# A two-layer decoder on one core: when expert lists are fetched, how constants are summed, and the order at the end of a feed-forward

## The chip, the cores and the metric

The kernel runs on one core of one Trainium2 chip. A core has TensorE (PE in the profile, with its weight loads as PEld), VectorE (DVE), ScalarE (ACT), GpSimd (POOL) and SyncE (SP), which here only issues transfers. The metric is the device time of one execution in microseconds. Before the change three runs gave a median of 3037.61 us (3037.56 to 3045.76).

## What is computed

A decoder of two layers works on x of shape (4, 512, 512): 4 batches, 512 tokens, 512 features. Each layer has self-attention, cross-attention and a feed-forward, and each of the six is added to x and normalised. The change lies in layer 0's feed-forward, a mixture of eight experts of which each token uses two:

```
h = x @ down_w + down_b
probs = softmax(x @ router_w + router_b - COST_LAMBDA * cost)
topv, topi = top_k(probs, 2);  gate = softmax(topv)
out = zeros
for k in range(2):
    mask = one_hot(topi[..., k], 8)
    acc = zeros
    for e, (w1, b1, w2, b2) in enumerate(experts):       # hidden sizes 256 512 768 1024, twice
        hm = h * mask[..., e:e + 1]
        acc = acc + (gelu(gelu(hm) @ w1 + b1) @ w2 + b2)
    out = out + acc * gate[..., k:k + 1]
out = out + 0.1 * (gelu(gelu(h) @ shared_w1 + shared_b1) @ shared_w2 + shared_b2)
out = out @ up_w + up_b
out = out + (gelu(x) @ core_w + core_b)
x = layernorm(x + out)
```

A token that an expert doesn't get still receives that expert's constant, `gelu(b1) @ w2 + b2`, as its masked input is zero. So the sum over all experts is one constant row, plus, for the two chosen experts, the difference between the true product and that constant.

## The kernel before, in words

All arithmetic around the change is in 32-bit floats; the trace shows each product of such operands as two matmul records ("passes"). The residual x stays in 16 tiles of 128 tokens by 512. PSUM tiles of one bank come from three rings that matter here: three `ps_s`, two `ps_t` (for transposes and small products), three `ps_m`.

The program is written in a tile language. A scheduler in it decides at compile time, from its own model, in which order each engine's queue holds its instructions: roughly source order, but an instruction that its model holds back is passed by later ones. Each engine then works through its own queue. The body of a runtime branch (`tc.If`) is scheduled as a block of its own. `mm` (L156, its matmuls are recorded at L160) and `add_projection` (L287, its adds at L292) are helpers used everywhere.

The feed-forward `l0_ffn` (L502) goes as follows.

- `hidden(b)` (L532) transposes a batch of x, makes `gelu(h)` for its 512 tokens and `gelu(x)`. `logits(b)` (L547) computes the router and a long chain of small VectorE operations: softmax, ranks, counts, gates. `send(b)` (L596) turns ranks into places and scatters each token's `gelu(h)` row to the lists of its two experts in HBM (`hidden_of`), by eight indirect transfers from GpSimd. `core(b)` (L627) adds `gelu(x) @ core_w` to the residual: 32 matmul passes of 512 columns, whose results VectorE adds to x (L292), four PSUM tiles a batch. `shared_expert(b)` (L681) is the expert that every token uses. The calls are written out from L742 on in the order hidden(0), logits(0), core(0), hidden(1), send(0), logits(1), shared_expert(0), hidden(2), send(1), logits(2), core(1), shared_expert(1), hidden(3), send(2), logits(3), shared_expert(2), send(3), the rotary angles, loads of experts 1 to 3, shared_expert(3).
- `add_bias` (L772) adds the output biases to x on GpSimd.
- The lists, from L776: expert e takes the first 512 rows of its list as one block. `fetch` (L697) loads them from HBM into the single buffer `ctx`, issued by SP and waiting for the scatters. `turn` (L707) transposes them (matmuls at L712, copies at L714 and L716). `block` (L733) runs the expert's hidden chunks of 128: `first(j)` (L636) multiplies by w1, ScalarE takes the gelu, VectorE subtracts gelu(b1); `second(j)` (L648, matmuls at L656) multiplies by w2 and accumulates. `run_pieces` (L671) puts each chunk's `second` behind the next chunk's `first`, so that TensorE has work while the gelu runs. Behind the second `first` of a block it calls `turn` for the next list. Results go back to HBM by SP (`store`, L719). The fetch of list e+1 is written ahead of block e.
- Behind every second expert there is a runtime branch (L793) for the rows past 512 of the two lists. It was entered for experts 6 and 7 only (the trace has their 384-row blocks between 918 and 963 us). Behind it stand the loads of the experts two pairs on (L804): after expert 1 those of 4 and 5, after expert 3 those of 6 and 7.
- `add_every(e)` (L736) adds expert e's constant to the row `every`: for each chunk of 128 hidden units one product of a single column of gelu(b1) with a 128x256 chunk of w2. In total 40 chunks.
- The end, from L806: `every` is turned into a column, GpSimd gathers each token's two result rows (32 indirect transfers, L817, eight a batch), `core(2)` and `core(3)` follow.
- `finish(b)` (L823) scales the first row by its gate on ScalarE (L827), adds the second on VectorE (L828), transposes, adds the constant and the shared expert (L833), projects by `up_w` onto x (16 passes) and normalises. `finish(0)` is called before layer 1's attention; that attention calls `finish(1)`, `finish(2)` and `finish(3)` after its heads 0, 1 and 2 (`at_start`).

Layer 1's attention, `l1_attn` (L843), runs 64 heads. While head n is finished, head n+1 is scored (`scores`, L893: product, causal mask, maximum, exponential) and the queries of head n+2 are projected and rotated (`queries`, `rope`; the last step of the rotation is on GpSimd, L860). `turn` (L913) transposes probabilities, `values` (L925) multiplies them by v and ends in a copy on ScalarE. A quarter of the time the keys of the next group are projected (`keys`, L875). `layernorm` (L215) takes bn_stats and bn_aggr of four tiles on VectorE, a root on ScalarE, a reciprocal and four scalings on VectorE.

Of the kernel before, what the change touches and what calls it, by code (L numbers as in the profile page):

```python
# [86 lines left out]
def decoder_kernel(ctx: ExitStack, tc: tile.TileContext, a: dict, out: bass.AP):  # L87
# [206 lines left out]
    def chunks(w):  # L294
        return [w[:, k, :] for k in range(w.shape[1])]
# [203 lines left out]

    def l0_ffn():  # L502
        slots = [cp.tile([P, T // P], I32, tag=f"slot{k}", name="slot") for k in range(2)]
        share = [cp.tile([P, T // P], F32, tag=f"share{k}", name="share") for k in range(2)]
# [8 lines left out]
        V.tensor_copy(b_down, ps[:, :L])  # L513
        G.tensor_tensor(cub, cub, ub, ALU.add)
        G.memset(run, 0.0)
        b1g = cp.tile([P, N_HCH], F32, tag="b1g", name="b1g")
        A.activation(b1g, bc[:, B_E1:B_E1 + N_HCH], AF.Gelu)
        gh, shared = [weight(), weight()], [weight(), weight()]
        base = {e: B_E1 + sum(HID[:e]) // P for e in range(N_EXP + 1)}
        st, rt, scatters, now = {}, {}, [], {}  # L520
# [213 lines left out]
            run_pieces(products(e, n, [y[:, :n] for y in x], store(e, start, n)), between)  # L734

        def add_every(e):  # L736
            w2 = experts[e][1]
            ps, at = pst(), base[e] - B_E1
            mm(ps[:1, :L], [b1g[:, at + i:at + i + 1] for i in range(w2.shape[1])], chunks(w2))
            V.tensor_tensor(every, every, ps[:1, :L], ALU.add)  # L740

        hidden(0)  # L742
        logits(0)
# [1 line left out]
        hidden(1)  # L745
        send(0)
        logits(1)
        shared_expert(0)
        hidden(2)
        send(1)  # L750
        logits(2)
        core(1)
        shared_expert(1)
        hidden(3)
        send(2)
        logits(3)
        b2 = ap.tile([N_EXP + 1, L], F32, tag="bias", name="b2", bufs=2)
        nc.sync.dma_start(b2, a["b2_rows"])

        every = prob("cos", [S], 1)[:1, :L]  # L760
        ps = pst()
        PE.matmul(ps[:1, :L], lhsT=kc[:N_EXP + 1, C_B2W:C_B2W + 1], rhs=b2, start=True, stop=True)
        V.tensor_copy(every, ps[:1, :L])
        shared_expert(2)
        send(3)
        all_angles()
# [6 lines left out]
            for x in X:  # L773
                G.tensor_tensor(x, x, cub, ALU.add)

        turned = {0: turn(fetch(0, 0, BLOCK), BLOCK)}  # L776
        add_bias()
        for e in range(N_EXP):
            ahead = {}
            if e + 1 < N_EXP:  # L780
                got = fetch(e + 1, 0, BLOCK)
                ahead[1] = lambda: turned.update({e + 1: turn(got, BLOCK)})
            block(e, 0, BLOCK, turned.pop(e), ahead)
            if 0 < e < N_EXP - 1:
                add_every(e + 1)
            if e % 2 == 0:
                continue
            flush()

            got = act("xT", [2, MORE // P, L])  # L790
            more = [fetch(e - 1 + i, BLOCK, MORE, got[:, i]) for i in range(2)]
            most, *count = nc.values_load_multi_w_load_instructions(counts[0:1, 3 * (e // 2):3 * (e // 2) + 3])[1]
            with tc.If(most > BLOCK):  # L793
                for i in range(2):
                    with tc.If(count[i] > BLOCK):
                        x = turn(more[i], MORE)
                        block(e - 1 + i, BLOCK, MORE, x)
                        flush()
                        with tc.If(count[i] > BLOCK + MORE):
                            for start in range(BLOCK + MORE, ROOM, MORE):  # L800
                                n = min(MORE, ROOM - start)
                                block(e - 1 + i, start, n, turn(fetch(e - 1 + i, start, n), n, x))
                                flush()
            experts.update((i, load_expert(i)) for i in range(e + 3, min(e + 5, N_EXP)))  # L804

        everyT = cp.tile([P, 2], F32, tag="everyT", name="everyT")  # L806
        for m in range(2):
            ps = pst()
            PE.matmul(ps[:, :1], lhsT=every[:, tk(m)], rhs=ones[:1, :1], start=True, stop=True)
            V.tensor_copy(everyT[:, m:m + 1], ps[:, :1])  # L810

        results = {}
        for b in range(B):
            y = results[b] = weight((4, 2, L))
            for t in range(4):
                for k in range(2):
                    G.indirect_dma_start(out=y[:, t, k, :], out_offset=None, in_=result_of[:],  # L817
                                         in_offset=bass.IndirectOffsetOnAxis(
                                             ap=slots[k][:, 4 * b + t:4 * b + t + 1], axis=0))
        core(2)  # L820
        core(3)

        def finish(b):  # L823
            y, o = results.pop(b), prob("ctx", [2, S], 1)
            for t in range(4):
                g1, g2 = (x[:, 4 * b + t:4 * b + t + 1] for x in share)
                A.activation(y[:, t, 0, :], y[:, t, 0, :], AF.Copy, scale=g1)  # L827
                V.scalar_tensor_tensor(y[:, t, 0, :], y[:, t, 1, :], g2, y[:, t, 0, :], ALU.mult, ALU.add)  # L828
            for m in range(2):
                pt = pst()  # L830
                for t in range(4):
                    PE.transpose(pt[:, tk(t)], y[:, t, 0, tk(m)], ident)
                V.scalar_tensor_tensor(o[:, m, :], pt, everyT[:, m:m + 1], shared[m][:, cols(b)],  # L833
                                       ALU.add, ALU.add)
            add_projection(b, chunks(o), chunks(up_w))
            layernorm(b)

        return finish

# [575 lines left out]
```

## Time and profile before

| what | us |
|---|---|
| median of three runs | 3037.61 |
| the profiled execution, whole | 3051.64 |
| its span, first to last instruction | 3049.9 |
| TensorE busy in it | 2851.6 (93%) |
| VectorE busy | 1770.6 (58%) |
| ScalarE busy | 1061.9 (35%) |
| GpSimd busy | 342.5 (11%) |
| hidden, logits, send, shared expert, cores 0 and 1 | about 583 to 718 |
| first blocks of the eight lists | about 718 to 917 |
| rows past 512 of lists 6 and 7 | about 917 to 966 |
| cores 2 and 3, finish of batch 0, first transposes of layer 1 | about 966 to 1031 |
| first heads of layer 1, finish of batches 1 to 3 | about 1031 to 1127 |

The busy time of an engine is summed over the whole span and says little about a stage; the stages above have their own limits. A line of a timeline gives start, duration, engine, source line, operation, output and inputs, and how many instructions are merged in it; the bracket at its end gives the idle time of the engine before it and what released it. A queue line (SPq) is the issue of a transfer, not the transfer. A row of the table by stage has, for each engine, the busy time and in parentheses the number of instructions; behind the engines follow the granted clock of TensorE (1.00 is full), the busy share of the 16 DMA engines and GB/s.

### The profile page before, as it was taken

How to read it: one execution, taken by the hardware profiler on the slowest of the kernel's cores; microseconds unless marked ns; L12 is line 12 of the kernel's file. 1: busy time of each engine (PE TensorE's matmuls, PEld its weight loads, DVE VectorE, ACT ScalarE, POOL GpSimd, SP SyncE). 2: the span in 40 equal slices, each digit the busy share in tenths (PEclk: the TensorE clock that was granted, in tenths of full speed). 3: DMA queues.
4: the chain of work that ended last, by engine and by line, in shares of the span. 5: the costliest groups of instructions: out<-in, count | busy, mean ns of one | idle time of the engine just before them, and what ended most of it. 6: DMA issues, size and time to landing. Idle time of an engine off the chain costs nothing.

```text
span 3049.9 us, 30386 instructions
## 1 busy us (share of the span) xinstructions
PE 2851.6 (93%) x11514; PEld 1370.0 (45%) x11514; DVE 1770.6 (58%) x3585; ACT 1061.9 (35%) x1945; POOL 342.5 (11%) x294
## 2 busy tenths in 40 slices
PE   7999998998798899999999999999899998998988
PEld 3444444565455345545545555533233343332444
DVE  4565455443111477757766766755655655564898
ACT  2343243233112222323322232334545444444444
POOL 3000000042002201101100100111212012110000
PEclk9999998989999899999999999999899898999999
DMA  9600001013312120000000001200201100000000
GB/s 374 266 15 1 18 11 35 11 39 115 122 38 77 55 83 1 1 1 1 1 1 1 1 28 35 90 1 15 90 1 42 63 1 28 1 15 1 1 28 28
DMA packets 56454, 131.85 MB, mean 43 GB/s; under 512 B 4810, under 2 KB 24027, under 8 KB 50147
## 3 DMA queue, kind: packets, MB, share of 16 engines
q1 hardware_dynamic: 53218, 121.31, 10.9%
q0 software_dynamic: 3072, 8.39, 0.8%
q8 instruction: 99, 1.62, 0.2%
q14 instruction: 65, 0.52, 0.1%
HBM read 82.76 MB, written 46.92 MB: 43 GB/s over the span
## 4 chain that ended last, share of the span: by engine, by line
PE 52%; DVE 10%; POOL 2%; issue 2%; DMA 1%; ACT 1%; POOLq 0%; DVEq 0%; ACTq 0%; SPq 0%
PE ps_m L160 19%; PE ps_b L1116 7%; PE ps_m L887 6%; PE ps_s L900 5%; PE ps_m L1143 4%; PE ps_b L1132 2%; PE ps_t L917 2%; PE ps_m L932 2%; POOL q L860 1%; DVE maxes L1120 1%; DVE P L1335 1%; PE ps_m L1095 1%; DMA w<-in_L_ffn_downT 1%; PE ps_s L160 1%; DVE tmp L859 1%
## 5 line engine op out<-in xcount | busy, mean ns | idle before, releaser
L160 PE MATMUL ps_m<-w,attnT 128*128 128x512 f32 (+2 forms) x1216 | 446.0, 517 | 12.3 <-issue 8.0
L1120 DVE TENSOR_REDUCE maxes<-ps_b 128x2 f32<-128x1024 f32 x256 | 311.1, 1222 | 244.5 <-PE ps_b L1132 223.6
L1136 ACT ACTIVATE PT<-ps_b 128x1024 f32<-128x1024 f32 x256 | 261.5, 1024 | 313.5 <-PE ps_b L1132 312.9
L1132 PE MATMUL ps_b<-q,k 32*128 32x512 f32 x1024 | 306.4, 678 | 33.3 <-DVE maxes L1120 33.3
L1116 PE MATMUL ps_b<-k,q 32*128 32x512 f32 x1024 | 310.3, 665 | 0.9 <-DVE maxes L1120 0.5
L160 PEld LDWEIGHTS ps_m<-w,attnT 128*128 128x128 f32 x960 | 182.9, 193 | 193.0 <-issue 177.3
L887 PE MATMUL ps_m<-xT,w 128*128 128x512 f32 x512 | 260.3, 592 | 0.0
L292 DVE TENSOR_TENSOR x<-x,ps_m 128x512 f32<-128x512 f32 x128 | 88.0, 688 | 247.5 <-PE ps_m L160 244.6
L904 ACT ACTIVATE P<-ps_s,nmax 128x512 f32<-128x512 f32 (+3 forms) x256 | 135.2, 529 | 233.5 <-DVE nmax L902 232.4
L900 PE MATMUL ps_s<-k,q 128*128 128x512 f32 (+3 forms) x512 | 183.4, 441 | 18.4 <-POOL q L860 18.1
L1116 PEld LDWEIGHTS ps_b<-k,q 32*128 32x128 f32 x1024 | 87.1, 193 | 177.4 <-issue 141.0
L860 POOL TENSOR_TENSOR q<-tmp 128x512 f32<-128x512 f32 x64 | 81.3, 1270 | 750.8 <-DVE tmp L859 714.8
L932 PE MATMUL ps_m<-PT,v 128*128 128x512 f32 (+3 forms) x512 | 162.0, 439 | 2.4 <-DVE PT L920 2.3
L349 ACT ACTIVATE P<-ps_s,nmax 128x512 f32<-128x512 f32 x128 | 88.5, 693 | 204.1 <-DVE nmax L347 204.1
L1143 PE MATMUL ps_m<-PT,vv 128*32 128x512 f32 x1024 | 148.8, 655 | 5.8 <-ACT PT L1136 5.7
L160 PE MATMUL ps_m<-w,xT 128*128 128x512 f32 (+1 forms) x384 | 144.8, 533 | 8.1 <-DVE xT L235 4.2
L911 DVE TENSOR_SCALAR P<-P,sums 128x512 f32<-128x512 f32 (+3 forms) x256 | 145.5, 571 | 4.6
L932 PEld LDWEIGHTS ps_m<-PT,v 128*128 128x128 f32 x512 | 89.0, 190 | 103.5 <-issue 49.7
L917 PEld LDWEIGHTS ps_t<-kc,P 128*128 128x128 f32 x640 | 84.0, 141 | 114.3 <-issue 84.3
L327 PE MATMUL ps_m<-xT,w 128*128 128x512 f32 x256 | 122.2, 604 | 11.1 <-DMA w<-in_L_attn_Wq 11.1
L902 DVE TENSOR_REDUCE nmax<-ps_s 128x1 f32<-128x512 f32 (+3 forms) x256 | 125.2, 490 | 5.1
L160 PE MATMUL ps_m<-xT,w 128*128 128x256 f32 (+1 forms) x384 | 124.9, 463 | 0.8 <-DVE x L292 0.8
(266 smaller groups left out, 4290.9 us busy)
## 6 DMA issues: line engine op xcount, KB each, us to landing
hidden<-w SPq DMA_DIRECT2D x16, 1024.0 KB, 18.8
result<-w SPq DMA_DIRECT2D x16, 1024.0 KB, 19.0
w<-in_L_ffn_gateT SPq DMA_DIRECT2D x8, 1024.0 KB, 4.9
w<-in_L_ffn_upT SPq DMA_DIRECT2D x8, 1024.0 KB, 4.8
w<-in_L_ffn_downT SPq DMA_DIRECT2D x8, 1024.0 KB, 5.1
w<-in_L_attn_Wqkv SPq DMA_DIRECT2D x6, 1024.0 KB, 6.0
w<-in_L_attn_Wo SPq DMA_DIRECT2D x5, 1024.0 KB, 9.2
result<-P SPq DMA_DIRECT2D x18, 256.0 KB, 2.1
```

What stands on the lines that cost most here:

```text
L160: PE.matmul(ps, lhsT=x, rhs=y, start=(i == 0), stop=(i == n - 1))
L887: PE.matmul(ps_q[n], lhsT=wq[h // 4][:, i, tk(h % 4)], rhs=st["xt"][:, i, :], start=(i == 0), stop=(i == 3))
L900: PE.matmul(s[:, :w], lhsT=q[:, tk(qi)], rhs=k[:, :w], start=True, stop=True)
L904: A.activation(p[:, :w], s[:, :w], AF.Exp, bias=nmax[:, qi:qi + 1], accum_out=sums[:, qi:qi + 1])
L911: V.tensor_scalar(p[:, :w], p[:, :w], sums[:, qi:qi + 1], None, ALU.mult)
L917: PE.transpose(pt[:, tk(qi)], probs[qi][:, tk(c)], ident)
L932: PE.matmul(av[:, c * P:], lhsT=st["v"][:, c, tk(g)], rhs=pts[c][:, c * P:], start=(c == 0), stop=(c == 3))
L1116: PE.matmul(s[:, j, :], lhsT=q[strip(i), tk(qi)], rhs=k[strip(i), :], start=True, stop=True)
L1120: V.tensor_reduce(at[:, 2 * half:2 * half + 2, 16 * (1 - g % 2)], s, AX.X, ALU.max, negate=True)
L1132: PE.matmul(s[:, j, :], lhsT=k[strip(i), tk(c)], rhs=q[strip(i), :], start=True, stop=True)
L1136: A.activation(p, s, AF.Exp)
L1143: PE.matmul(avs[g][strip(i), :], lhsT=vv[c][:, 4 * m + i, 16 * par:16 * par + 32], rhs=pts[g, c, i // 2][:, i % 2, :], start=(c == 0), sto ...
```

## The change

Five edits in `l0_ffn`, one in how its end is scheduled.

1. `shared_expert(0)` is called behind `core(1)` instead of behind `logits(1)`, and `shared_expert(1)` behind `logits(3)` instead of behind `core(1)`.
2. `add_every` puts chunk i into the column strip i mod 4 of TensorE: 32 columns from column i of gelu(b1) on, so that row 32*(i mod 4) of the PSUM tile gets the chunk's product and the other 31 rows of the strip get products that nobody reads. The tile of gelu(b1) is 31 columns longer, cleared by GpSimd. `every` has 128 rows, cleared once by VectorE; up to four of them, a strip apart, hold partial sums.
3. The final transposition of `every` multiplies by a column that is 1 in the rows 0, 32, 64 and 96, which adds the partial sums.
4. A list is fetched right behind the `turn` of the preceding list, inside the preceding block, instead of ahead of the next block. In the branch for more than 896 rows, which was not entered, the rows go to another buffer than `ctx`.
5. `core(3)` is called inside `finish(0)`, behind its layernorm, instead of ahead of `finish(0)`.
6. From `core(2)` to the layernorm of batch 3 the queues of TensorE, VectorE and ScalarE are held in source order. The stretch contains `finish(0)`, `core(3)`, the start of layer 1's attention and its heads 0 to 2 with `finish(1)` to `finish(3)`. GpSimd and SP stay with the scheduler.

```
+    in_order = ExitStack()
...
-        b1g = cp.tile([P, N_HCH], F32, tag="b1g", name="b1g")
-        A.activation(b1g, bc[:, B_E1:B_E1 + N_HCH], AF.Gelu)
+        b1g = cp.tile([P, N_HCH + 31], F32, tag="b1g", name="b1g")
+        G.memset(b1g[:, N_HCH:], 0.0)
+        A.activation(b1g[:, :N_HCH], bc[:, B_E1:B_E1 + N_HCH], AF.Gelu)
...
         def add_every(e):
+
             w2 = experts[e][1]
-            ps, at = pst(), base[e] - B_E1
-            mm(ps[:1, :L], [b1g[:, at + i:at + i + 1] for i in range(w2.shape[1])], chunks(w2))
-            V.tensor_tensor(every, every, ps[:1, :L], ALU.add)
+            ps, at, nj = pst(), base[e] - B_E1, w2.shape[1]
+            for i in range(nj):
+                r = slice(32 * (i % 4), 32 * (i % 4) + 32)
+                PE.matmul(ps[r, :L], lhsT=b1g[:, at + i:at + i + 32], rhs=w2[:, i, :],
+                          start=(i < 4), stop=(i + 4 >= nj))
+            n = 32 * min(nj, 4)
+            V.tensor_tensor(every[:n], every[:n], ps[:n, :L], ALU.add)
...
         logits(1)
-        shared_expert(0)
         hidden(2)
         send(1)
         logits(2)
         core(1)
-        shared_expert(1)
+        shared_expert(0)
         hidden(3)
         send(2)
         logits(3)
+        shared_expert(1)
...
-        every = prob("cos", [S], 1)[:1, :L]
+        every = prob("cos", [S], 1)[:, :L]
+        V.memset(every, 0.0)
...
-        V.tensor_copy(every, ps[:1, :L])
+        V.tensor_copy(every[:1], ps[:1, :L])
...
-        turned = {0: turn(fetch(0, 0, BLOCK), BLOCK)}
+        turned, got = {}, {0: fetch(0, 0, BLOCK)}
+
+        def turn_next(e):
+            if e < N_EXP:
+                turned[e] = turn(got.pop(e), BLOCK)
+                if e + 1 < N_EXP:
+                    got[e + 1] = fetch(e + 1, 0, BLOCK)
+
+        turn_next(0)
         add_bias()
         for e in range(N_EXP):
-            ahead = {}
-            if e + 1 < N_EXP:
-                got = fetch(e + 1, 0, BLOCK)
-                ahead[1] = lambda: turned.update({e + 1: turn(got, BLOCK)})
-            block(e, 0, BLOCK, turned.pop(e), ahead)
+            block(e, 0, BLOCK, turned.pop(e), {1: lambda: turn_next(e + 1)})
...
-            got = act("xT", [2, MORE // P, L])
-            more = [fetch(e - 1 + i, BLOCK, MORE, got[:, i]) for i in range(2)]
+            rest = act("xT", [2, MORE // P, L])
+            more = [fetch(e - 1 + i, BLOCK, MORE, rest[:, i]) for i in range(2)]
...
-            PE.matmul(ps[:, :1], lhsT=every[:, tk(m)], rhs=ones[:1, :1], start=True, stop=True)
+            PE.matmul(ps[:, :1], lhsT=every[:, tk(m)], rhs=kc[:, C_ROW1:C_ROW1 + 1], start=True, stop=True)
...
+        in_order.enter_context(tc.manual_schedule(engines={nc.tensor.engine, nc.vector.engine, nc.scalar.engine}))
         core(2)
-        core(3)
...
             layernorm(b)
+            if b == 0:
+                core(3)
+            if b == B - 1:
+                in_order.close()
```

More of the change, by code (lines that the diff above doesn't have):

```diff
@@ L801, in l0_ffn @@
                                 n = min(MORE, ROOM - start)
-                                block(e - 1 + i, start, n, turn(fetch(e - 1 + i, start, n), n, x))
+                                block(e - 1 + i, start, n, turn(fetch(e - 1 + i, start, n, rest[:, i]), n, x))
                                 flush()
```

## The prediction, made before the changed kernel was built or run

> **What bounds the kernel now.** I read the page first, then the busy time by stage, then TensorE's timeline in the feed-forward, and for each gap there the queue it waited on. The page says TensorE carries the kernel: 93% busy. By stage, that breaks down once:
>
> ```profile
> 718.00:917.00 199.00, 170.50 (x606) 106.50 (x607) 32.50 (x62) 37.04 (x56) 0.00 (x0) 0.93 0.28 93
> 966.00:1031.00 65.00, 48.34 (x109) 21.51 (x110) 23.40 (x47) 11.04 (x21) 30.39 (x32) 0.86 0.41 136
> 1031.00:1127.00 96.00, 92.79 (x284) 46.76 (x284) 70.29 (x169) 28.79 (x65) 9.48 (x8) 0.99 0.19 66
> ```
>
> The columns are stretch, length, busy time of PE, PEld, DVE, ACT, POOL, then granted clock. TensorE is idle 28.5 of 199 us in the expert lists and 16.7 of 65 us at the feed-forward's end; then, in the first heads of layer 1, which finish batches 1 to 3, only 3.2 of 96. In the lists four gaps hold 26.3 us: before `turn` of lists 0 (6.15), 3 (5.28), 5 (10.43) and 7 (4.40). The queue of loads shows why for list 5:
>
> ```profile
> 820.93 3.62 PE L656 MATMUL ps_s<-w,k 128*128 128x256 f32 x16
> 834.98 1.94 PE L712 MATMUL ps_t<-kc,ctx 128*128 128x128 f32 x8 [10.43 <-DMA ctx<-hidden]
> 836.85 2.98 PE L160 MATMUL ps_t<-w,b1g 128*1 128x256 f32 x8
> ```
>
> ```profile
> 821.14 0.37 SPq L490 DMA_DIRECT2D w<-in_L_ffn_e_w  x1
> 821.62 0.41 SPq L491 DMA_DIRECT2D w<-in_L_ffn_e_w  x1
> 822.08 0.54 SPq L490 DMA_DIRECT2D w<-in_L_ffn_e_w  x1
> 822.66 0.66 SPq L491 DMA_DIRECT2D w<-in_L_ffn_e_w  x1
> 823.42 3.29 SPq L701 DMA_DIRECT2D ctx<-hidden  x1
> ```
>
> The list is fetched behind 3.5 MB of weights for experts 6 and 7. A gap costs more than itself: the eight passes at 834.98 take 1.94 us where eight elsewhere take 1.04. Stretches of 2 us show why, in the third column from the end: the granted clock falls to half about 4 us into the gap and stays there in the first work behind it.
>
> ```profile
> 825.00:827.00 2.00, 0.00 (x0) 0.00 (x0) 0.28 (x1) 0.00 (x0) 0.00 (x0) 1.00 1.06 373
> 829.00:831.00 2.00, 0.00 (x0) 0.00 (x0) 0.00 (x0) 0.00 (x0) 0.00 (x0) 0.50 1.04 363
> 835.00:837.00 2.00, 2.00 (x9) 1.60 (x10) 0.04 (x1) 0.59 (x1) 0.00 (x0) 0.50 1.09 384
> ```
>
> The end of the stage:
>
> ```profile
> 966.55 10.57 PE L160 MATMUL ps_m<-w,v 128*128 128x512 f32 x24
> 977.49 3.70 PE L160 MATMUL ps_m<-w,v 128*128 128x512 f32 x8 [0.37 <-issue]
> 984.56 5.40 PE L160 MATMUL ps_m<-w,attnT 128*128 128x512 f32 x8 [3.37 <-issue]
> 992.16 5.40 PE L160 MATMUL ps_m<-w,attnT 128*128 128x512 f32 x8 [2.19 <-DVE w L828]
> 1002.23 5.40 PE L160 MATMUL ps_m<-w,attnT 128*128 128x512 f32 x8 [4.67 <-issue]
> 1009.67 5.40 PE L160 MATMUL ps_m<-w,attnT 128*128 128x512 f32 x8 [2.04 <-DVE w L828]
> ```
>
> `core(3)` crawls because VectorE's adds, which free its PSUM tiles, stand between the combines (L828) of all four batches, and these wait for gathers that GpSimd issues every 1.25 us until 1009.2.
>
> **The change, part by part** (us of this execution).
>
> *Constants in strips.* After list 0 has started, `add_every` runs six times: 68 passes of 256 columns, measured start to start 2.68 for 12 and 3.54 for 16, so 0.22 each, 15.2 in all, on TensorE's path. The nearest row for strips is layer 1's `values`, also 128 rows by 32 columns, with 512 columns moving:
>
> ```profile
> 2200.68 1.06 PE L1143 MATMUL ps_m<-PT,vv 128*32 128x512 f32 x8
> 2201.67 0.70 PE L1116 MATMUL ps_b<-k,q 32*128 32x512 f32 x2
> ```
>
> Eight passes take 0.99 start to start, so four chunks of 256 columns about 0.5. With 6, 8, 2, 4, 6, 8 chunks: 1.0+1.0+0.45+0.5+1.0+1.0 = 5.0. Saved 10.2; 7.7 if a pass can't follow sooner than a strip's weight load (0.11 each, 7.5), 11 at best. [...] But the strips above start between two other tilings, 0.07 before the modelled end of the pass ahead, so I take 10.2. VectorE's add stays near 0.41 on more partitions; the two clears are one short instruction each.
>
> *Lists fetched behind the preceding turn.* The fetch needs only the `ctx` buffer, which the preceding `turn` frees (lists 0 to 2 are fetched as now: 1 and 2 leave right behind that turn already, at 725.97 and 732.39). On SP it moves ahead of the block's stores, the pair's branch and extra fetches; while it waits for the turn's 0.9 us of transposes, those stores stand behind it, and nobody waits for a store before the gathers at 969. Lists 3, 5, 7 are then asked for a whole block earlier, ahead of the weight loads too; a list lands 3.7 after its issue (median), and each now has over 10. What goes is gap plus slow clock after it: 5.28+1.5, 10.43+2.1, 4.40+2.9 = 26.6. What is late next is list 6: its fetch follows the turn of list 5, about 4.6 after block 4 begins (817.43 before), on SP behind the same weights (issued 3.7 to 5.9 after), so it lands where list 5 landed, 17.5 after. It is needed after two firsts, a turn, two seconds, `add_every`, first, second, first: 3.5+0.9+3.5+0.5+5.2, about 13, or 12 if block 4's last second runs under block 5. So 0 to 7.6 comes back (5.5 and its slow clock); the scheduler may put the rest of block 5, 10 us of matmuls, before that turn, so I take 4. Net 22.6.
>
> *Shared expert moved back, list 0.* No work is added; one shared block, about 8.5, moves from before `logits(3)` to behind it. List 0's chain (send at 702.7, scatters 705.2 to 715.6, landing 724.0) is 21.3 long and starts behind `shared_expert(2)` either way. With another block to cover VectorE's routing, the angles' product (0.95), pulled ahead of the send now, and a slow first product (4.90 at 693.28 where eight such passes take 3.70) need not lie before it: about 2 earlier. The gap before list 0 widens instead, as one shared block still follows the send and `add_every(0)`, `(1)` shrink under it: their 2 saved count for nothing. Bounds: 5 lost (VectorE's L594 took 4.60 under GpSimd's bias adds at 636; that can land elsewhere) to 6 gained. I take 2.
>
> *The end.* In source order `core(2)` runs unhindered, 966.55 to 980.3. Batch 0's gathers are in by 981.0, its combines end at 983.1, transposes and L833 at 985.1; projection 6.9 plus slow clock ends near 993. `core(3)`, 13.75, covers the layernorm (about 7 after the projection) and ends at 1006.8; the turns put layer 1's keys at 1009.4 to 1012.8, against an end of 1035.6 before: 22.8 gained. SP's weight loads for layer 1 wait for the tiles that these steps free, so they move forward too. But source order runs on until batch 3's layernorm, within heads 0 to 2, and there it takes cover away. Smaller: the fourth score of head 0 needs a PSUM tile freed by an exponential: 1.7. Larger: each `finish`. In source order ScalarE's scalings follow the copy of the head's values, so after the head's last matmul: copy 0.65, four scalings to 2.9, last combine 3.4, transposes, two L833 to 5.2; TensorE's projection starts at 4.5, of which 3.6 is idle. Before, scalings and combines were long done. Then four bn_stats follow the last residual add: 3.6, root and reciprocal 0.5, scalings 1.95, so VectorE is 7 us late for the next head's masks; TensorE has 5.3 of head work until the third turn needs a tile that ScalarE frees at 9.4, and the late rope holds up the last values matmul: 4.8 in all. Slow clock: [...] after 2.19 and 2.04 idle, eight passes took 5.40 against 3.70. I take 1.9. Batch 1: 3.6+1.9+4.8+1.0 = 11.3; batch 2: 9.0, since `keys(4)` (3.44) fills part; batch 3: 4.5, as order is free again behind it. Sum 24.8, less 2.2 idle there before: 22.6. The end nets 22.8-1.7-22.6, 1.5 lost; bounds from 14 gained (a finish at 3 each, as if the combines slipped in) to 10 lost.
>
> Sum: 10.2+22.6+2-1.5 = 33.3. The profiled execution took 3051.6 (span 3049.9 and 1.7 around it), so 3018.3; the median of the runs is 14.0 lower, 3037.6, so 3004.3.
>
> **Rivals.**
> *The end is a clear gain.* Speaks for it: 3.2 idle in 96 us before, so the engines have room; against: the order above. 15.5 more: 2989.
> *The waits only move*, to lists 6 and 0 in full: 10.2+19-5-1.5 = 22.7: 3015. For it: the 3.5 MB stay; against: matmuls to put before the turn.
> *The strips don't run together*: 3014.5; the `values` row speaks against it.
> *Source order in the heads costs more than all the gains: slower.* All but the finishes gains 10.2+22.6+2+22.8-1.7+2.2 = 58.1 (2.2: today's idle there, part of each finish's price), so it decides from 19.4 per finish. With nothing beneath layernorm, first softmax and rope, and one stall of 4.6 as at L594, a finish comes to 3.6+1.9+7+2.4+2.1+4.6, about 22: 66-58, 8 lost: 3046. Against it: 5.3 of head work remains.
>
> **How the numbers follow.** Main case 3004 (0.48), clear gain at the end 2989 (0.22), waits move 3015 (0.18), strips 3014 (0.06), slower 3046 (0.06). The first four with their bounds span 2984 to 3024. A measurement tells about 0.3%, 9 us, from no change: faster 0.87, same 0.07 (far ends of waits and finishes together), slower 0.06.
>
> **What would show it.** Right: no gap before turns 3, 5, 7; a gap up to 5.5 at list 6; add_every 0.5 to 1.0 long; layer 1's keys ending some 47 us after the last list's work, not 70; gaps near 4 before each finish's projection and in the head after it. Wrong: no gaps in heads 0 to 2 (then faster), or a gap over 7 at list 6 or over 11 at list 0, or combines of later batches still between core's adds.

## The result, and the profile after

The changed kernel took 2999.69 us (median of 4 runs, 2996.43 to 3003.11) against 3041.69 for the kernel before (4 runs beside it): a ratio of 0.986, 95% interval 0.9834 to 0.9886, 42.0 us less. Forecast were 33.3 less. Two later repeats on other chips gave 0.9922 (0.9896 to 0.9948) and 0.9892 (0.9866 to 0.9918), 27 and 35 us less; why they differ is part of what follows.

The profiled execution of after took 3003.11 (span 3001.3), 48.5 less than that of before. By stage, each from one landmark in TensorE's queue to the next:

| stage | before | after | saved |
|---|---|---|---|
| start of the feed-forward | at 581.41 | at 574.57 | 6.8, ahead of any changed line |
| to the first `turn` (list 0) | 142.59 | 133.78 | 8.8 |
| to `core(2)` (lists, branches) | 242.55 | 210.45 | 32.1 |
| to the first queries of layer 1 | 69.08 | 44.04 | 25.0 |
| to the scores behind head 3's projection | 103.53 | 125.17 | -21.6 |
| to the end | 1910.7 | 1913.3 | -2.6, unchanged code |

The first and last rows are noise of single executions: in fourteen profiles of kernels with the same code there, the start lies at 574.4 to 581.8 and the last stage takes 1899.6 to 1913.4. So the stages between are compared with each other, and whole times only by ratio to the kernel before on the same chip, or by medians of one chip.

The busy time by stage, for the stretches that correspond to the three shown of before (the first columns are stretch, length and TensorE's busy time; behind the five engines follows the granted clock):

```profile
702.00:870.00 168.00, 159.09 (x628) 100.55 (x627) 34.08 (x66) 37.71 (x59) 0.00 (x0) 0.99 0.33 111
918.00:958.00 40.00, 37.78 (x100) 17.36 (x100) 16.72 (x33) 3.79 (x7) 27.61 (x29) 1.00 0.55 180
958.00:1076.00 118.00, 104.52 (x294) 50.97 (x292) 78.84 (x181) 34.67 (x79) 13.29 (x12) 0.93 0.19 67
```

TensorE is idle 8.9 us in the lists where it was 28.5, and 2.2 at the end where it was 16.7. In the heads it is idle 13.5 where it was 3.2, at a clock of 0.93 where it was 0.99. TensorE's timeline in the lists:

```profile
756.06 1.07 PE L746 MATMUL ps_t<-w,b1g 128*32 128x256 f32 x16
757.07 1.99 PE L160 MATMUL ps_m<-PT,w 128*128 128x512 f32 x4
...
762.33 1.04 PE L716 MATMUL ps_t<-kc,ctx 128*128 128x128 f32 x8
...
785.69 0.63 PE L746 MATMUL ps_t<-w,b1g 128*32 128x256 f32 x4
...
789.85 3.67 PE L160 MATMUL ps_m<-PT,w 128*128 128x512 f32 x8 [1.62 <-PEq L807]
...
793.36 1.04 PE L716 MATMUL ps_t<-kc,ctx 128*128 128x128 f32 x8
...
796.06 0.64 PE L746 MATMUL ps_t<-w,b1g 128*32 128x256 f32 x8
...
807.77 1.81 PE L716 MATMUL ps_t<-kc,ctx 128*128 128x128 f32 x8 [3.13 <-DMA ctx<-hidden]
```

Behind the constants of 16 passes the next work starts after 1.01, where it started after 3.54. List 5 is turned at 793.36 with no wait in front, where it waited 10.43; the only wait for a list left here is 3.13 before list 6, fetched at 794.73 right behind the weights of experts 6 and 7. The end:

```profile
918.80 13.98 PE L160 MATMUL ps_m<-w,v 128*128 128x512 f32 x32
934.03 1.95 PE L846 MATMUL ps_t<-kc,w 128*128 128x128 f32 x8 [1.25 <-DVE w L842]
936.39 7.13 PE L160 MATMUL ps_m<-w,ctx 128*128 128x512 f32 x16 [0.41 <-DVE ctx L847]
943.36 13.90 PE L160 MATMUL ps_m<-w,attnT 128*128 128x512 f32 x32
...
962.84 7.03 PE L905 MATMUL ps_m<-xT,w 128*128 128x512 f32 x16
```

`core(2)`, the finish of batch 0 and `core(3)` follow each other with only 1.25 and 0.41 us of idle between, and `core(3)` takes 13.90 instead of crawling from 984.56 to 1014.9. And in the heads, finish 1 and the head after it:

```profile
999.56 2.43 PE L846 MATMUL ps_t<-kc,w 128*128 128x128 f32 x8 [1.70 <-DVE w L842]
1001.98 9.09 PE L160 MATMUL ps_m<-w,ctx 128*128 128x512 f32 x16
...
1019.66 0.69 PE L935 MATMUL ps_t<-kc,P 128*128 128x128 f32 x2 [3.32 <-ACT PT L940]
```

The transposes wait for the combines, the projection takes 9.09 where an undisturbed one takes 7.13, and the third turn of the next head waits 3.32.

### The profile page after: what moved, and what is told of

Its sections match the earlier page's. It is cut to its first block, busy times and chain, and to the rows that moved or that the text cites. A ratio compares the mean times of both kernels' runs of the same rounds, so it can differ in the third digit from the quotient of the medians.

```text
span 3001.3 us, 30363 instructions
## 1 busy us (share of the span) xinstructions
PE 2827.6 (94%) x11492; PEld 1361.0 (45%) x11514; DVE 1772.1 (59%) x3586; ACT 1058.6 (35%) x1944; POOL 342.4 (11%) x295
## 3 DMA queue, kind: packets, MB, share of 16 engines
q1 hardware_dynamic: 53218, 121.31, 11.1%
q8 instruction: 99, 1.62, 0.2%
## 4 chain that ended last, share of the span: by engine, by line
PE 53%; DVE 11%; POOL 2%; issue 1%; ACT 1%; DMA 1%; another core or an unknown queue 0%; POOLq 0%; DVEq 0%; ACTq 0%; SPq 0%
PE ps_m L160 19%; PE ps_b L1134 8%; PE ps_m L905 6%; PE ps_s L918 5%; PE ps_m L1161 4%; PE ps_b L1150 3%; PE ps_m L950 2%; PE ps_t L935 2%; DVE maxes L1138 1%; POOL q L878 1%; DVE P L1353 1%; PE ps_m L1113 1%; PE ps_s L160 1%; DVE tmp L877 1%; DVE tmp L876 1%
## 5 line engine op out<-in xcount | busy, mean ns | idle before, releaser
L160 PE MATMUL ps_m<-w,attnT 128*128 128x512 f32 (+2 forms) x1205 | 438.0, 513 | 0.5
L292 DVE TENSOR_TENSOR x<-x,ps_m 128x512 f32<-128x512 f32 x128 | 87.9, 687 | 267.2 <-PE ps_m L160 267.0
L160 PE MATMUL ps_m<-PT,w 128*128 128x512 f32 (+1 forms) x248 | 116.9, 601 | 10.9 <-DVE PT L691 5.2
## 6 DMA issues: line engine op xcount, KB each, us to landing
result<-w SPq DMA_DIRECT2D x16, 1024.0 KB, 16.7
```

Source lines behind the costliest of these rows:

```text
L160: PE.matmul(ps, lhsT=x, rhs=y, start=(i == 0), stop=(i == n - 1))
```

## The experiments

All are edits of the changed kernel unless it says otherwise. Each series ran on a chip of its own, beside the kernel before.

**First series: undo one part.** The reference:

> The changed kernel once more, unaltered, as the reference of the three runs below. Its ratio to the kernel before was 0.986 (2999.7 against 3041.7). If the gain is in the stages of the feed-forward alone, the ratio is 0.986 to 0.988 (the stages that the change touches sum to 43.4 saved less the 6.8 that arose before any changed line does not enter). If the 6.8 that the profile shows ahead of the first changed line, at a granted clock of 0.93 against 0.86, belongs to the change, the ratio stays under 0.985 and that stretch is short again.

3016.7 us, ratio 0.9922 (0.9896 to 0.9948), neither of the two outcomes that were expected. The 6.8 us ahead of the feed-forward were gone again (start at 580.19): noise. The stages up to `core(2)` agree with the first profile (133.93 and 210.11), the heads too (125.11), but the stage from `core(2)` to the first queries took 61.7 instead of 44.0, with waits inside `core(3)`. In this timeline of TensorE and VectorE (other lines left out) L292 is the add of a finished PSUM tile to x:

```profile
941.82 7.43 PE L160 MATMUL ps_m<-w,ctx 128*128 128x512 f32 x16 [0.41 <-DVE ctx L847]
...
946.52 0.69 DVE L292 TENSOR_TENSOR x<-x,ps_m 128x512 f32<-128x512 f32 x1 [4.10 <-PE ps_m L160]
...
950.75 0.69 DVE L292 TENSOR_TENSOR x<-x,ps_m 128x512 f32<-128x512 f32 x1 [3.54 <-PE ps_m L160]
...
959.85 0.69 DVE L292 TENSOR_TENSOR x<-x,ps_m 128x512 f32<-128x512 f32 x1 [8.41 <-remote]
...
960.59 5.39 PE L160 MATMUL ps_m<-w,attnT 128*128 128x512 f32 x8 [5.40 <-DVE x L292]
...
969.68 0.69 DVE L292 TENSOR_TENSOR x<-x,ps_m 128x512 f32<-128x512 f32 x1 [9.14 <-remote]
...
970.42 5.40 PE L160 MATMUL ps_m<-w,attnT 128*128 128x512 f32 x8 [4.44 <-DVE x L292]
```

The 16 passes of the projection are recorded by 949.25, four a tile, and in the first profile the four adds follow them at 938.41, 940.13, 941.84 and 943.56. Here the last add starts at 969.68, 20 us after its passes. VectorE isn't busy: each of these adds waits for one semaphore, TensorE's signal that the tile is done. TensorE in turn waits for the add, as `core(3)` needs the tile back. The semaphore times in the trace say the same: in the first profile TensorE's signal follows the recorded end of the pass by 0.02 us, here by 2.7, 5.2, 12.6 and 20.4.

`e_no_strips`, `add_every` as before:

```
-            for i in range(nj):
-                r = slice(32 * (i % 4), 32 * (i % 4) + 32)
...
+            mm(ps[:1, :L], [b1g[:, at + i:at + i + 1] for i in range(w2.shape[1])], chunks(w2))
+            V.tensor_tensor(every[:1], every[:1], ps[:1, :L], ALU.add)
```

> add_every as it was before (one output row, passes one after the other); all else as changed. Theory (strips are worth their passes on TensorE's path): 9 to 10 us slower than the changed kernel, with the six calls behind list 0 at 15 us instead of 5.1. Rival (the shorter passes only fill waits that other work sets, above all the 3.1 us before list 6): 4 to 6 slower, and that wait is gone. Lists stay without a wait at 3, 5 and 7 under both.

3027.5, ratio 0.9949 (0.9929 to 0.9969): 8.2 us slower than the reference by the ratios (0.0027 of 3043.9; 10.8 by the medians), with intervals that overlap, so the stage is the firmer number. The stage of the lists took 216.48, 6.4 more. The six calls take 15.2 again, 10.1 more, and 2.3 of that fills waits: the branch's wait in front of `block(2)` was 1.62 and is 0.65, that in front of `block(6)` 1.75 and 0.47; the remaining 1.4 has no single place. So neither holds whole: the stage lies just above the rival's 4 to 6, but the wait before list 6, which the rival had go, stays (2.68).

`e_late_fetch`, the fetches at their old place in the source:

```
-            block(e, 0, BLOCK, turned.pop(e), {1: lambda: turn_next(e + 1)})
+            ahead = {}
+            if e + 1 < N_EXP:
+                got = fetch(e + 1, 0, BLOCK)
+                ahead[1] = lambda: turned.update({e + 1: turn(got, BLOCK)})
+            block(e, 0, BLOCK, turned.pop(e), ahead)
```

> Lists fetched as before, ahead of the next block and behind the branch and its two further fetches; all else as changed. Theory (the place of the fetch makes the waits): waits of 4 to 10 us return before the turns of lists 3, 5 and 7, each with slow passes behind it, the wait of 3.1 before list 6 goes, 19 to 24 us slower than the changed kernel. Rival (the waits went because the strips and the bias work moved the lists in time): under 8 slower, at most one wait over 3.

3021.7, ratio 0.9918 (0.9896 to 0.9940); the stage of the lists took 210.39 against 210.11. Not one wait came back at lists 3, 5 and 7:

```profile
744.14 1.04 PE L716 MATMUL ps_t<-kc,ctx 128*128 128x128 f32 x8
...
766.87 1.04 PE L716 MATMUL ps_t<-kc,ctx 128*128 128x128 f32 x8
...
794.93 5.37 PE L160 MATMUL ps_m<-PT,w 128*128 128x512 f32 x8 [2.15 <-PEq L803]
...
800.13 1.04 PE L716 MATMUL ps_t<-kc,ctx 128*128 128x128 f32 x8
...
812.13 1.09 PE L716 MATMUL ps_t<-kc,ctx 128*128 128x128 f32 x8 [0.72 <-DMA ctx<-hidden]
...
824.25 3.67 PE L160 MATMUL ps_m<-PT,w 128*128 128x512 f32 x8 [2.09 <-PEq L803]
...
827.76 1.04 PE L716 MATMUL ps_t<-kc,ctx 128*128 128x128 f32 x8
```

The theory fell. The rival's number holds, but not its reason: with the strips undone, too, lists 3, 5 and 7 didn't wait. The wait before list 6 shrank to 0.72, but eight passes behind a branch took 5.37 instead of 3.67. The fetch of list 5, which is turned at 800.13, stands in SyncE's queue at

```profile
767.94 0.36 SPq L705 DMA_DIRECT2D ctx<-hidden  x1
```

27 us ahead of the branch behind which it is written: the scheduler moved it there. What this kernel still shares with the change is the one line in the branch's innermost body, which no longer uses `ctx`.

`e_shared_back`, `shared_expert(0)` and `(1)` at their old places:

> shared_expert(0) and (1) at their places of before, the rest as changed. Theory (the move let the scheduler start send(3) ahead of half a shared block, so that list 0 arrives with TensorE still busy): 7 to 10 us slower than the changed kernel, and a wait of about 6 before list 0 returns. The prediction on record, which has the chain of list 0 start behind shared_expert(2) either way: 0 to 4 slower. Rival (the 8.8 us of that stage come from the clock of the one profiled run): no difference, within 3 us.

3028.8, ratio 0.9946 (0.9927 to 0.9966): 7.3 slower than the reference by the ratios (12.1 by the medians); the stage to the first `turn` took 142.25 against 133.93, 8.3 more, and list 0 waited 7.51 again. The theory's number holds. In the changed kernel the send's products stand ahead of the second half of a shared block:

```profile
686.05 0.30 PE L160 MATMUL ps_t<-t,kc 128*128 128x32 f32 x2
...
687.76 3.70 PE L664 MATMUL ps_s<-k,w 128*128 128x512 f32 x8
...
697.03 6.22 PE L160 MATMUL ps_m<-PT,w 128*128 128x512 f32 x8 [4.69 <-DVE PT L691]
...
708.35 0.66 PE L716 MATMUL ps_t<-kc,ctx 128*128 128x128 f32 x4
```

and with the old order behind it:

```profile
699.13 3.70 PE L664 MATMUL ps_s<-k,w 128*128 128x512 f32 x8
702.67 0.30 PE L160 MATMUL ps_t<-t,kc 128*128 128x32 f32 x2
...
723.63 1.94 PE L716 MATMUL ps_t<-kc,ctx 128*128 128x128 f32 x8 [7.51 <-DMA ctx<-hidden]
```

From send to `turn` it is 22.3 in the one and 21.0 in the other: the chain is no shorter, it starts earlier, 111.5 us into the stage instead of 121.3. The half block accounts for 3.5 of these 9.8 and the angles' product, now behind the send too, for 1.0. Most of the rest is a wait of TensorE's: with the old order it stands idle 4.17 at 641.67 in `hidden(2)` (4.16 at 641.69 before the change), held up behind a VectorE step of 4.6 on 128x4 values, which runs while GpSimd adds biases. With the new order such a step takes 4.87 at 628.00, and TensorE doesn't wait for it. The 4.69 in the first fence stands behind the send, under the chain. So the theory names about half of the cause.

The size goes with the granted clock, too: with TensorE's instructions in the same order this stage took 133.8 to 133.9 in five profiles (granted clock 0.89 over its first 130 us) and 130.6 to 130.7 in five others (0.92).

**Second series.** `b_rest` is the kernel before with that one line of the change (and the name `rest` for the buffer that it takes):

```
-    block(e - 1 + i, start, n, turn(fetch(e - 1 + i, start, n), n, x))
+    block(e - 1 + i, start, n, turn(fetch(e - 1 + i, start, n, rest[:, i]), n, x))
```

> The kernel before with one line of the change alone: the fetch inside the innermost branch (lists over BLOCK+MORE) writes the buffer of the extra pieces instead of the single ctx buffer. The fetches stay where they were in the source. Theory, formed after the late-fetch run kept its lists without waits: it was this use of ctx inside the branch that held every later fetch behind the branch, so the waits before lists 3, 5 and 7 (5.3, 10.4, 4.4) and their slow passes go, 2 to 3 come back at list 6: 18 to 24 us faster than before. The prediction on record (the place of the fetch in the source makes the waits): within 3 us of before, waits unchanged.

3026.4 against 3049.3, ratio 0.9922 (0.9906 to 0.9939): 22.9 us faster, by the medians, by a line in a branch that is not entered. The stage of the lists took 222.52 against 242.55. Its turns:

```profile
755.35 1.04 PE L712 MATMUL ps_t<-kc,ctx 128*128 128x128 f32 x8
...
780.63 1.04 PE L712 MATMUL ps_t<-kc,ctx 128*128 128x128 f32 x8
...
808.23 3.67 PE L160 MATMUL ps_m<-PT,w 128*128 128x512 f32 x8 [1.29 <-PEq L793]
...
811.74 1.04 PE L712 MATMUL ps_t<-kc,ctx 128*128 128x128 f32 x8
...
828.41 1.97 PE L712 MATMUL ps_t<-kc,ctx 128*128 128x128 f32 x8 [5.43 <-DMA ctx<-hidden]
...
844.37 3.70 PE L160 MATMUL ps_m<-PT,w 128*128 128x512 f32 x8 [0.40 <-ACTq L793]
...
847.91 1.04 PE L712 MATMUL ps_t<-kc,ctx 128*128 128x128 f32 x8
```

Lists 3, 5 and 7 don't wait; 5.43 stands before list 6. The fetch of list 5, at 823.42 before, now stands ahead of the branch and its weights:

```profile
781.70 0.36 SPq L701 DMA_DIRECT2D ctx<-hidden  x1
```

Lists 3, 5 and 7 are just those whose fetch is written behind a branch. There the branch's own fetch was the next user of the single `ctx` buffer, so theirs had to come after it.

`e_plain_rows` leaves the gather of batches 1 to 3 out, and with it the right rows, so its result isn't the decoder's:

```
+            if b:
+                for k in range(2):
+                    at = (2 * b + k) * ROOM
+                    nc.sync.dma_start(y[:, :, k, :], result_of[at:at + S, :].rearrange("(t p) n -> p t n", p=P))
+                continue
```

> The changed kernel, in which the rows of batches 1 to 3 are not gathered by index: fixed rows of the same size come through SyncE's queue (this leaves out the gather of 24 of 32 row groups, and the output with it). Theory (TensorE's completion signals come late while GpSimd issues indirect DMAs: in the repeat of the changed kernel the four tiles of the first projection reported 2.7 to 20 us after their passes, in the first profile of it none did): core(3) runs without the waits of 2.3, 5.4 and 4.4, the stage from core(2) to layer 1's first queries takes 44 to 46 instead of 61.7, and the kernel is 14 to 18 us faster than the repeat of the changed one. Rival (VectorE's order or the loads of layer 1's weights make those waits): 58 to 62, no more than 4 faster.

3000.9, ratio 0.9833 (0.9809 to 0.9858); 47.05 to the first queries, without waits in `core(3)`. But on this chip no signal came late in any of the four kernels, also in the three in which the gathers stayed. So the run doesn't tell the two theories apart.

`e_close_early` ends the source order behind `core(3)`:

```
             if b == 0:
                 core(3)
-            if b == B - 1:
                 in_order.close()
```

> The changed kernel with the source order ended right behind core(3), so that finishes 1 to 3 and the heads are ordered by the scheduler again. Theory (source order in the first heads costs about 21 against before): the stage from layer 1's first queries to the scores behind head 3's projection takes 103 to 108 instead of 125, and the kernel is 14 to 20 faster than the changed one. Rival (a finish in the heads costs the same in whichever order, and what was saved before was paid in front of the keys): over 120, or the time comes back ahead of the queries, no more than 5 faster.

2994.1, ratio 0.9831 (0.9811 to 0.9851). The changed kernel wasn't run on this chip; its first ratio, 0.986 (0.9834 to 0.9886), overlaps, so the verdict is by stages. The heads took 103.53, exactly as before the change; but the stage ahead of them took 67.79. Together 171.3, where the first profile of the changed kernel has 169.2. The rival's second half happened: once the finishes are free, the scheduler puts combines of later batches ahead of batch 0's, where in the kernel before they stood ahead of `core(3)`'s adds:

```profile
954.82 2.51 PE L846 MATMUL ps_t<-kc,w 128*128 128x128 f32 x8 [20.45 <-DVE w L842]
...
957.32 6.93 PE L160 MATMUL ps_m<-w,ctx 128*128 128x512 f32 x12
```

`e_split_finish` keeps the order and splits each finish: `combine(n + 1)` ahead of head n's scores, and

```
+            if 0 < n < 4:
+                layernorm(n)
             values(n, pts)
```

> The changed kernel, source order kept, with each finish of batches 1 to 3 split: scalings and combines ahead of the head's scores, projection behind the head as now, layernorm only behind the next head's masks and turns. Theory (a finish's price is the idle before its transposes, the slow passes behind it, and the late masks of the next head): about 1.7 and 2.0 per finish and 3.3 and 1.9 in the heads go, 8 to 14 us faster than the changed kernel in the stage of the heads. If only the layernorm ahead of the masks counts: 5 to 6. Rival (the price is the projection itself and the exchange of PSUM tiles): under 3.

3001.4, ratio 0.9840 (0.9825 to 0.9856); the heads took 124.50 against 125.17, so the rival's number. The reason isn't the rival's: the waits of 1.70, 3.32 and 1.89 went, and two of 6.56 came in their place, each with slow passes behind it (16 take 9.91 and 10.01 instead of 7.13):

```profile
1030.89 3.78 PE L160 MATMUL ps_m<-w,ctx 128*128 128x512 f32 x4 [6.56 <-DVE ctx L850]
```

L850 is the VectorE step between a finish's transposes and its projection; it now stood behind the layernorm's bn_stats, root and scalings. A layernorm in VectorE's fixed order has to stand ahead of something.

**Third series.** `e_late_share` frees the heads and keeps the combines out of `core(3)` by data, as their shares are copied behind it:

```
-                g1, g2 = (x[:, 4 * b + t:4 * b + t + 1] for x in share)
+                g1, g2 = (x[:, 4 * b + t:4 * b + t + 1] for x in (later if b else share))
...
             if b == 0:
                 core(3)
-            if b == B - 1:
+                for k in range(2):
+                    V.tensor_copy(later[k][:, 4:], share[k][:, 4:])
                 in_order.close()
```

> The changed kernel with the source order ended right behind core(3), and with the scalings and combines of batches 1 to 3 reading a copy of the shares that VectorE makes behind core(3)'s last add, so that the scheduler can't put them ahead of core(3). Theory (what the order is worth is that these combines stay out of core(3), and what it costs is that finishes 1 to 3 stand in source order in the heads): the stage from core(2) to layer 1's first queries takes 44 to 49, as with the order, and the heads 103 to 107, as without: 17 to 23 us faster than the changed kernel. Rival (the two are one sum: whatever leaves core(3) comes back in the heads): 165 to 171 for both stages together, no more than 4 faster.

`e_best` also loads the weights of experts 6 and 7 later:

```
                     got[e + 1] = fetch(e + 1, 0, BLOCK)
+                    if e == 5:
+                        experts.update((i, load_expert(i)) for i in (6, 7))
...
-            experts.update((i, load_expert(i)) for i in range(e + 3, min(e + 5, N_EXP)))
+            if e == 1:
+                experts.update((i, load_expert(i)) for i in (4, 5))
```

> The same, and the weights of experts 6 and 7 are loaded behind the fetch of list 6 instead of ahead of it. Theory (these 3.5 MB ahead of the fetch make the wait of 2.4 to 3.1 before list 6 and the slow passes behind it): that wait goes, 3 to 5 us faster than the run without this step, unless the weights then come late for expert 6, which would show as a wait of its first products. Rival (the wait is the fetch's own way, 3.7 us from issue to landing, behind stores): no difference, within 1.5.

The references on this chip are the changed kernel and `e_end_back`, the changed kernel with the end of before:

> The changed kernel a third time, as the reference of this chip. If TensorE's completion signals come late here while GpSimd issues its indirect DMAs (as in the four runs of the first call), the stage from core(2) to the first queries takes 60 to 63 and the ratio to before is 0.990 to 0.993; if not (as in its first profile and in the four runs of the second call), 44 to 45 and 0.985 to 0.988.

> The end of before (core(3) right behind core(2), no source order), all else as changed. Theory (the end is nearly a draw: 25 gained ahead of the queries, 21.6 lost in the heads): 0 to 6 us slower than the changed kernel where its signals come in time; 10 to 15 faster where they come late, since then the changed kernel loses 17 in core(3), which the end of before spends waiting for the combines anyway. Stages: 66 to 70 to the first queries, then 103 to 104. The prediction on record: 1.5 us faster than the changed kernel.

```
-        in_order.enter_context(tc.manual_schedule(engines={nc.tensor.engine, nc.vector.engine, nc.scalar.engine}))
         core(2)
+        core(3)
...
-            if b == 0:
-                core(3)
-            if b == B - 1:
-                in_order.close()
```

| kernel | median us | ratio to before | 95% interval | to `core(2)` | to the queries | heads |
|---|---|---|---|---|---|---|
| before | 3045.27 | | | | | |
| changed (`e_after_again`) | 3010.23 | 0.9892 | 0.9866 to 0.9918 | 210.51 | 58.18 | 124.78 |
| `e_end_back` | 2998.04 | 0.9847 | 0.9824 to 0.9870 | 211.35 | 68.26 | 103.54 |
| `e_late_share` | 3000.55 | 0.9851 | 0.9829 to 0.9873 | 211.00 | 62.41 | 104.95 |
| `e_best` | 2989.41 | 0.9817 | 0.9794 to 0.9840 | 206.48 | 58.03 | 104.95 |

On this chip the signals came late again, and the changed kernel lost 14 us up to the queries (58.18 against 44.04). So here the end of before is the faster by 12 by the medians (11.2 by the two stages), as its `core(3)` waits for combines in the meantime anyway. `e_late_share` has the heads at 104.95, as its theory said; its first stage shows the late signals, so what it would be without them wasn't measured. Its two stages sum to 167.4, which the rival allowed (165 to 171), but the sum of the changed kernel on this chip is 183.0, so the heads were not paid for again. It is 9.7 faster than the changed kernel by the medians (12.5 by the ratios), where its theory had 17 to 23. `e_best` lost the wait at list 6, 4.5 in the stage:

```profile
804.95 1.04 PE L716 MATMUL ps_t<-kc,ctx 128*128 128x128 f32 x8
```

In SyncE's queue the fetch of list 6 now stands between the weights of expert 6 and those of expert 7. It has the lowest ratio to the kernel before of those run here, and is 20.8 faster than the change on its chip by the medians. Of its 11.1 against `e_late_share`, 4.5 lies in the lists and 4.4 in the stage with the late signals, so only the first is surely its own.

## Why the prediction was right, and where it was not

The total came out near the forecast of 3004 partly by luck: of its four parts, the lists have the right size with a wrong cause, and the shared expert has a quarter of its size.

**Strips: right.** Forecast 10.2, from 15.2 to 5.0; the calls take 5.1. Seen from the path it is 6 to 8, since part of the old passes filled the branch's wait. Laid in strips, passes of 0.22 would take 0.44 for the calls with 2 and 4 chunks and 0.88 for the others (an estimate from the old passes); start to start the two short calls take 0.55 and 0.57 and the four others 0.99 to 1.01, so 0.11 to 0.13 more than that each, some 0.7 in all. VectorE's add of a call takes 0.41 to 0.42 on 64 or 128 partitions, where it took 0.41 on one.

**Lists: the size right, the cause wrong.** Forecast 22.6; the two edits of that part are worth 20.0 by `b_rest`'s stage and 22.9 by its time. The step that failed is "The fetch needs only the `ctx` buffer, which the preceding `turn` frees", read as if the place in the source decided. The inner branch's fetch was a further user of `ctx`, and that line alone makes the gain; the moved fetch is worth nothing that can be measured (210.39 against 210.11). The list of edits above names the line; the sum gave it no part, so that the number came out right is luck. What comes back at list 6 was rightly sized: 4 against 3.13 and 0.8 of slow passes. The parts don't add up singly: 20.0 by `b_rest` and 6.4 by `e_no_strips` leave 5.7 of the stage's 32.1 to neither. `b_rest` waits 5.43 before list 6, where the changed kernel waits 3.13, at a granted clock of 0.96 against 0.98 in the stage.

**Shared expert: mis-sized.** Forecast 2, bounds -5 to 6; 8.8 by the profiles and 8.3 by undoing it. The step that failed is that the chain of list 0 "starts behind `shared_expert(2)` either way": it starts ahead of that block's second half. The prediction did name the VectorE step of 4.60 at 636, but only as something that could land elsewhere and cost 5; it already held TensorE up for 4.16 ahead of the send, and that wait is gone.

**The end: right in the first comparison, not everywhere.** Counted from `core(2)`, layer 1's keys end 25.0 earlier (forecast 22.8), the heads lose 21.6 (forecast 24.3 with the fourth score), net 3.4 gained against 1.5 lost. But the profile of before has late signals and that of after none. `b_rest`, which has the end of before and no late signals, takes 66.42 and 103.53, 170.0 together, so like against like the net is 0.7: a draw, and nothing of the 14 that the rival of a clear gain had. Within a finish the idle before the transposes is 1.70, not 3.6, as TensorE starts behind the first combine, not behind the last; but the transposes then take 2.43, and the projection starts 4.1 behind the head's last pass, where 4.5 was forecast. The slow clock (0.50 from 1000 to 1004) costs 2.0 by the projection alone (9.09 against 7.13), the head after it 3.32, not 4.8. "`core(3)`, 13.75" is the term that fails on two chips, where late signals add 14 to 18; on the one of them where the end was undone it is a loss of 11, and the whole gain falls to 27 to 35 us. The profile of before has the late signals too (one tile of `core(3)` ended at 1007.62 and was reported at 1014.20), but it waits for the combines anyway: `b_rest`, without them, is only 2.7 shorter there. The slow rival was far off: three finishes cost 21.6, some 7 each, and it decides from 19.4.

The sum of the first comparison: 33.3, 6.8 more for the shared expert, 4.9 more at the end, 0.7 less in the lists and strips, 4.2 of noise at start and end are the 48.5 between the profiles. By the medians it is 42.0.

Of the slow clock: in the gap before list 5 of the kernel before it fell to half (0.50 from 829 on) about 4 us into the idle time. Here it fell after less, in stretches of 2 us of the changed kernel (third column from the end):

```profile
998.00:1000.00 2.00, 0.44 (x2) 0.32 (x2) 1.93 (x6) 2.00 (x5) 0.34 (x1) 0.78 0.00 0
1000.00:1002.00 2.00, 2.00 (x9) 1.17 (x8) 1.35 (x3) 1.37 (x2) 0.00 (x0) 0.50 0.00 0
1002.00:1004.00 2.00, 2.00 (x3) 0.97 (x4) 0.75 (x1) 0.00 (x0) 0.00 (x0) 0.50 0.40 112
1004.00:1006.00 2.00, 2.00 (x4) 0.86 (x3) 0.20 (x1) 0.00 (x0) 0.00 (x0) 0.51 0.95 347
1006.00:1008.00 2.00, 2.00 (x6) 0.86 (x5) 0.81 (x2) 0.00 (x0) 0.00 (x0) 1.00 0.20 74
```

The longest idle there is 1.70; TensorE was busy 0.44 of the 2 us in which the clock begins to fall (0.78). The prediction's 1.9, an estimate from two rows of before with 2.19 and 2.04 of idle ahead of them, stands against 2.0 measured. The clock was full again (1.00) from 1006 to 1008, behind some 6 us of unbroken work from 1000 on, in which it was 0.50 to 0.51.

## What to carry to other kernels

Before crediting a moved transfer, list every user of its buffer in program order, those in branches that never run included; the scheduler moves a transfer by itself once nothing stands between. An order written out by hand doesn't remove a conflict between two steps, it chooses who pays. A data dependency that holds back the one step that must not pass (here the later combines) leaves the rest free: the heads went from 124.78 to 104.95, and the two stages were 4.4 shorter than with the end of before on that chip (167.4 against 171.8). And repeat a profile on another chip before a stage is called settled.

## What the runs showed of the hardware

TensorE's signals of finished tiles can come late, in the repeat by 2.7 to 20.4 us. In nine of the fourteen profiles some of them lag or are missing from the trace, and only in stretches in which GpSimd issues indirect transfers (scatters around 620 to 716, gathers around 925 to 970; the profile of before is one of the nine, with gathers until 1009). In the other five, the first profile of the changed kernel and the four of the second series, every signal follows its pass by 0.02 us, though four of these issue the same transfers. Within the first and the third series all four kernels had it, so it goes by chip or by session, not by kernel. Nor is it TensorE's alone: against its first profile, the repeat of the same kernel has 11 fewer semaphore updates of TensorE (2525 of 2536), 39 of VectorE (3123 of 3162) and 10 of ScalarE (1460 of 1470), and GpSimd's 225 are all there. That the passes were not merely slow is suggested by the repeat: with two tiles of `core(3)` outstanding, two signals came 0.09 us apart, though a tile needs 3.7 of passes. It isn't the adds being blocked: each takes 0.69 once released. What holds the signals back stays open: the run without gathers fell on a chip without lag, so it isn't shown that the indirect transfers cause it, they only coincide with it. Whether the lag comes with the recording of the profile, which lacks updates in just these nine, was not tested either.
